# Graph and feed-forward stack on one core: the order of loads, stores and layer tiles in the first stage

## The chip, the cores and the metric

The kernel runs on one core of a Trainium2 chip. The metric is device time in microseconds (us) of one execution. A core has a matrix engine (PE, whose weight loads are listed apart as PEld), a vector engine (DVE), an activation engine (ACT), a general engine (POOL) and a synchronisation engine (SP). Transfers between device memory (DRAM) and on-chip memory are issued here from the queues of SP, ACT and POOL, and are carried out by 16 DMA engines. Each engine runs its own instructions in order. Times in the profile count from the start of the profiled span, and L12 is line 12 of the kernel.

## The reference

Four graph layers and four feed-forward blocks follow each other on 625 nodes with 512 features. Each adds its result to `x`. Only the first graph layer concerns the change:

```python
edge_index = jnp.stack([src, dst])
x = x + _L0_gnn_ref(_layernorm(x, axis=-1), edge_index, L0_gnn_W, L0_gnn_b)
x = x + _L0_ffn_ref(_layernorm(x, axis=-1)[None], ...)[0]
...
def _L0_gnn_ref(x, edge_index, W, b):
    loops = jnp.arange(n, dtype=edge_index.dtype)
    row = jnp.concatenate([edge_index[0], loops])
    col = jnp.concatenate([edge_index[1], loops])
    deg = jax.ops.segment_sum(jnp.ones(row.shape[0]), row, num_segments=n)
    dis = jax.lax.rsqrt(deg)
    norm = dis[row] * dis[col]
    h = x @ W.T + b
    out = jax.ops.segment_sum(norm[:, None] * h[row], col, num_segments=n)
    return jax.nn.relu(out)
```

There are 10,000 edges. Later graph layers use the same edges: one with the edge weights, one with the mean over the incoming edges, one with the degrees of the target nodes on both sides.

## The kernel before, in words

The 625 nodes are five tiles (`NT`) of 125 (`P`) partitions, and `x` stays on chip as `x[125, 5, 512]`. The 10,000 edges lie as 80 on each of 125 partitions. The kernel turns the edges into dense matrices of 625 by 625, `count` (number of edges) and `weighted` (sum of weights), and every graph layer is then a matrix product. The first stage, `graph_and_L0_gnn` (L369), runs in this order:

1. Loads. `Ctx.__init__` issues the load of `x` on SP's queue (L67). Then come `src` on SP (L387), `dst` on ACT (L388), the edge weights on SP (L390), the layer's weight (L464, issued by the helper at L92) and its bias (L98, on ACT).
2. Edges. DVE turns the indices into sorting keys (L392 to L409). `sort(t)` (L422) picks with MAX8 and MATCH_REPLACE8 up to 32 edges (`CAP`) of each partition whose source lies in tile t.
3. Matrices. For each tile and each of 32 slots DVE makes one-hot rows (`hot_dst` L477, `hot_src` L470), ACT makes three weighted copies of the latter (L472), and PE multiplies them into `wide` and `rest` (L497, L499). That is 640 pairs of matmuls. The sort of the next tile, and in the first tile the layer norm of `x` (`C.layernorm(xn, C.x)`, L487; its statistics are L152), are put between them.
4. A branch for left-over edges (L517) that every engine has to pass. `weighted` is stored for later (L554).
5. The tail. `degrees` makes 1/sqrt of the degrees. `turn(t)` transposes the normed `x` on PE (L609). `source_row` (L585) spreads the degrees over a row. `symmetric` (L576) makes one tile of a normalised matrix on DVE (L578, L580). `hidden(t)` is `x W + b` (PE L230, bias added by DVE, L615). `targets` (L561) sums `count` over columns on PE (L564) into `drow` (ACT L566). `layer(t)` (L619) multiplies `m0` with all five tiles of `h` (PE L213), and DVE adds the result to `x` (L622) and takes statistics (L623). `mean` (L569) makes the mean matrix (DVE L570, L571, POOL L573) and stores it (L574). `target_row` and `target_col` (L595, L599) and five more `symmetric` make `sym`, which is stored at L646. The order of the calls is written out at L625 to L647: hidden tiles, targets, then the five layer tiles with mean, target_row, target_col and sym between them.
6. The next stage, `L0_ffn` (L650), places its tiles in on-chip memory that the first stage's pool has given back. It loads expert weights into a ring (L676), norms `x` into `xn` (L161), transposes it (L173), and makes q, k, v (L237, L230) and an attention of 20 turns (L262 to L366).

The order of instructions on an engine is not quite the program's: the framework plans each engine's order with times of its own, taking what it believes ready and, among that, what stands earlier in the program. The trace shows this, for instance where DVE does L152 of the layer norm ahead of L64 and L392. Once planned, the order is fixed, and an instruction whose data is late holds up all behind it on its engine. PSUM tiles of the tail come from one pool of three buffers, named `pt`.

The three stored matrices are `[125, 5, 625]` in float32, 1525.9 KB each. Their stores go out as one transfer of 125 partitions; the later loads of the same matrices are already split in two, 112 and 13 partitions (`load_graph`, L203).

Of the kernel before, what the change touches and what calls it, by code (L numbers as in the profile page):

```python
# [28 lines left out]
N, D, P, NT = 625, 512, 125, 5  # L29
KC = D // 128  # L30
HALVES = ((0, 313), (313, 312))
# [17 lines left out]
class Ctx:  # L49


    def __init__(self, tc, ins, out, stack):
        self.tc, self.nc, self.ins, self.out = tc, tc.nc, ins, out
        nc = tc.nc
        pool = lambda name, bufs, **k: stack.enter_context(tc.tile_pool(name=name, bufs=bufs, **k))
        self.keep = pool("keep", 1)
        self.dram = pool("scratch", 1, space=DRAM)
        self.stack = stack
        self.open_mid("right")
        part = self.keep.tile([128, 1], F32, name="part")  # L60
        nc.gpsimd.iota(part, pattern=[[0, 1]], base=0, channel_multiplier=1,
                       allow_small_or_imprecise_dtypes=True)
        self.ident = self.keep.tile([128, 128], F32, name="ident")
        nc.vector.tensor_scalar(self.ident, self.iota[:, :128], part, None, op0=ALU.is_equal)  # L64
        self.ones = self.keep.tile([128, 128], F32, name="ones")
        nc.vector.memset(self.ones, 1.0)
        nc.sync.dma_start(self.x, ins["x"].rearrange("(t p) d -> p t d", p=P))  # L67

        self.graph = {
            k: self.dram.tile([P, NT, N], F32, name=f"graph_{k}") for k in ("weighted", "mean", "sym")  # L70
        }
# [130 lines left out]

    def load_graph(self, pool, kind):  # L203
        m = pool.tile([P, NT, N], F32, name=f"m_{kind}")

        for a, b in ((0, 112), (112, P)):
            self.nc.sync.dma_start(m[a:b], self.graph[kind][a:b])
        return m

    def aggregate(self, out, m, t, h, start=True, stop=True):  # L210

# [157 lines left out]
def graph_and_L0_gnn(C):  # L369
# [9 lines left out]
    nc, tc, I = C.nc, C.tc, C.ins  # L379
    W0, W1 = 512, N - 512  # L380
    with ExitStack() as st:
        E = st.enter_context
        pool = E(tc.tile_pool(name="g", bufs=1))
        T = lambda shape, name, dtype=F32: pool.tile(shape, dtype, name=name)
# [3 lines left out]
        nc.scalar.dma_start(ints[:, 1], I["dst"].rearrange("(p c) -> p c", p=P))  # L388
        ew = T([P, EC], "edge_w")
        nc.sync.dma_start(ew, I["edge_weight"].rearrange("(p c) -> p c", p=P))  # L390
        iota = T([P, N], "iota16", F16)
        nc.vector.tensor_copy(iota, C.iota[:P])  # L392
        ef = T([P, 2, EC], "edge_f")
# [67 lines left out]
        count, weighted = T([P, NT, N], "count"), T([P, NT, N], "weighted")  # L461
# [89 lines left out]
        drow, inv, trow, srow = (T([P, N], k) for k in ("drow", "inv", "trow", "srow"))  # L551
        m, sym, m0 = (T([P, NT, N], k) for k in ("m", "sym", "m0"))
        xT = T([128, KC, N], "xT")
        nc.sync.dma_start(C.graph["weighted"], weighted)  # L554


        def degrees():
# [3 lines left out]
        def targets(n0, w_):  # L561
            pr = ps.tile([128, 512], F32, name="pt")
            for s in range(NT):
                nc.tensor.matmul(pr[:P, :w_], C.ones[:P, :P], count[:, s, n0:n0 + w_],  # L564
                                 start=s == 0, stop=s == NT - 1)
            nc.scalar.copy(drow[:, n0:n0 + w_], pr[:P, :w_])  # L566


        def mean():  # L569
            nc.vector.tensor_scalar_max(inv, drow, 1.0)  # L570
            nc.vector.reciprocal(inv, inv)  # L571
            for t in range(NT):
                nc.gpsimd.tensor_mul(m[:, t], count[:, t], inv)  # L573
            nc.sync.dma_start(C.graph["mean"], m)  # L574

        def symmetric(m, t, sq, col, row):  # L576

            nc.vector.scalar_tensor_tensor(m[:, t], count[:, t], col[:, t:t + 1], row, op0=ALU.mult, op1=ALU.mult)  # L578
            diag = m[:, t, t * P:(t + 1) * P]
            nc.vector.scalar_tensor_tensor(diag, C.ident[:P, :P], sq[:, t:t + 1], diag, op0=ALU.mult, op1=ALU.add)  # L580
# [4 lines left out]
        def source_row(t):  # L585
            if t == 0:
                nc.vector.tensor_mul(ssq, scol, scol)
            dg = C.small.tile([P, P], F32, name="junk")
            nc.vector.tensor_scalar(dg, C.ident[:P, :P], scol[:, t:t + 1], None, op0=ALU.mult)
            pr = ps.tile([128, 512], F32, name="pt")  # L590
            nc.tensor.matmul(pr[:P, :P], C.ones[:P, :P], dg, start=True, stop=True)
            nc.scalar.copy(srow[:, t * P:(t + 1) * P], pr[:P, :P])


        def target_row():  # L595
            nc.vector.tensor_scalar_add(drow, drow, 1.0)
            C.rsqrt(trow, drow, [P, N])

        def target_col():  # L599
            for t in range(NT):  # L600
                junk = C.small.tile([P, P], F32, name="junk")
                nc.vector.scalar_tensor_tensor(junk, C.ident[:P, :P], 1.0, trow[:, t * P:(t + 1) * P],
                                               op0=ALU.mult, op1=ALU.mult, accum_out=tcol[:, t:t + 1])
            nc.vector.tensor_mul(tsq, tcol, tcol)
# [7 lines left out]
        def hidden(t):  # L612
            ph = ps.tile([128, 512], F32, name="pt")
            C.linear(ph[:P], xT, t, w)
            nc.vector.tensor_add(h[:, t], ph[:P], bias[:P])  # L615
# [3 lines left out]
        def layer(t):  # L619
            po = ps.tile([128, 512], F32, name="pt")  # L620
            C.aggregate(po[:P], m0, t, h)
            nc.vector.scalar_tensor_tensor(C.x[:, t], po[:P], 0.0, C.x[:, t], op0=ALU.max, op1=ALU.add)  # L622
            nc.vector.bn_stats(C.stats[:, t], C.x[:, t])  # L623
# [3 lines left out]
            turn(t)  # L627
        for t in range(NT):
            source_row(t)
        for t in range(NT):  # L630
            symmetric(m0, t, ssq, scol, srow)
            hidden(t)
        for n0, w_ in HALVES:
            targets(n0, w_)
        layer(0)
        mean()
        layer(1)
        target_row()
        layer(2)
        target_col()  # L640
        for t in (0, 1):
            symmetric(sym, t, tsq, tcol, trow)
        layer(3)
        for t in range(2, NT):
            symmetric(sym, t, tsq, tcol, trow)
        nc.sync.dma_start(C.graph["sym"], sym)  # L646
        layer(4)  # L647


def L0_ffn(C):  # L650
# [1094 lines left out]


PHASES = [graph_and_L0_gnn, L0_ffn, L1_gnn, L1_ffn, L2_gnn, L2_ffn, L3_gnn, L3_ffn]


# [48 lines left out]
```

## Time and profile before

| What | us |
|---|---|
| Median of three runs | 5357.06 |
| Lowest and highest | 5355.81, 5363.99 |
| The profiled execution's own time | 5365.64 |
| Span of its trace | 5363.8 |
| PE busy in the span | 4975.2 (93%) |
| DVE busy | 2690.5 (50%) |
| ACT busy | 1100.6 (21%) |
| First matmul starts | 27.14 |
| First PE work of `L0_ffn` starts | 280.66 |

In the page's listing, a line of the timeline has the start, the busy time, the engine, the line, the operation, the written and read tiles with their shapes, how many instructions were merged (x5), and in brackets the idle time of the engine just before it and who ended it. A letter q after an engine's name stands for its queue: the time given there is that of issuing the transfer, not of the transfer. The table by windows gives busy time and number of instructions for each engine, the granted PE clock (1.00 is full), the mean share in which the 16 DMA engines were busy, and GB/s. PE is busy through most of the span, but the averages say nothing of the first stage, which is the first twentieth of it and has its own gaps.

### The profile page before, as it was taken

The numbers are of one execution on the slowest core, as the hardware profiler recorded it, in microseconds if no ns is written. First come the engines' busy times: TensorE is split into PE (matmuls) and PEld (weight loads), VectorE is DVE, ScalarE is ACT, GpSimd is POOL, SyncE is SP. The second block draws the span as 40 slices with busy tenths as digits, with TensorE's granted clock in tenths as the row PEclk, the third lists the DMA queues.
The fourth block names the chain that finished last, engine by engine and source line by source line (L and its number), as shares of the span: only waits on it lengthen the run. The fifth ranks groups of instructions, "written<-read, shape, count | busy, mean of one in ns | idle before, by whom it ended". The sixth has DMA issues, their size and how long they took to land. (4 is left out here: it accounts for less than half of the span.)

```text
span 5363.8 us, 184920 instructions
## 1 busy us (share of the span) xinstructions
PE 4975.2 (93%) x74524; PEld 3140.2 (59%) x74524; DVE 2690.5 (50%) x13552; ACT 1100.6 (21%) x4478; POOL 61.6 (1%) x57
## 2 busy tenths in 40 slices
PE   7986999999999979999999999999999999999988
PEld 5555755555556645555555555565555655555545
DVE  6533024240025146666666656666566666656258
ACT  7433111110115111111111111111111111111125
POOL 0000000000000000000000000000000000000000
PEclk9987998989989989999999999999999999999988
DMA  1031962221116310000000000000000000000100
GB/s 37 34 109 55 319 191 73 89 65 53 45 50 214 124 39 6 7 11 6 6 6 6 6 6 6 6 6 12 7 6 6 6 6 6 6 6 0 54 27 10
DMA packets 167915, 232.19 MB, mean 43 GB/s; under 512 B 64226, under 2 KB 80983, under 8 KB 167000
## 3 DMA queue, kind: packets, MB, share of 16 engines
q1 hardware_dynamic: 155388, 220.04, 12.9%
q10 hardware_dynamic: 10122, 7.55, 0.5%
q0 software_dynamic: 2240, 2.57, 0.2%
q8 instruction: 81, 1.33, 0.1%
q14 instruction: 84, 0.69, 0.0%
HBM read 196.59 MB, written 33.54 MB: 43 GB/s over the span
## 5 line engine op out<-in xcount | busy, mean ns | idle before, releaser
L1496 PE MATMUL pa<-wp,left 128*23 128x384 bf16 x33312 | 1502.7, 327 | 129.7 <-issue 39.2
L1496 PEld LDWEIGHTS pa<-wp,left 128*23 128x23 bf16 x33312 | 811.0, 93 | 643.9 <-DVE left L1633 153.9
L1525 PE MATMUL po<-wo,left 128*1 128x128 f32 x20000 | 659.1, 273 | 0.0
L1525 PEld LDWEIGHTS po<-wo,left 128*1 128x1 f32 x20000 | 482.7, 84 | 126.6 <-issue 0.2
L1537 PE MATMUL spare<-wo,ident 128*128 128x256 f32 x1250 | 437.4, 431 | 25.2 <-issue 25.2
L1611 DVE STREAM_TRANSPOSE col<-pa 128x384 f32<-128x384 f32 x625 | 349.3, 559 | 194.5 <-PE pa L1496 194.5
L1601 DVE COPY col<-gxb 128x16 f32 x625 | 114.4, 183 | 652.0 <-DVEq L1576 652.0
L1568 ACT ACTIVATE act<-ga 128x12 f32<-128x12 f32 x625 | 132.7, 212 | 1185.7 <-DVE ga L1613 1185.7
L1563 ACT COPY xrow<-xsb 1x4 f32<-1x4 f32 x625 | 120.5, 193 | 1211.4 <-ACTq L1561 1211.4
L1537 PEld LDWEIGHTS spare<-wo,ident 128*128 128x128 f32 x1250 | 186.1, 188 | 165.7 <-issue 165.7
L1338 PE MATMUL pg<-xT,w 128*128 128x312 f32 (+1 forms) x1024 | 275.2, 429 | 1.4 <-DVE gt L1347 0.7
L1338 PEld LDWEIGHTS pg<-xT,w 128*128 128x128 f32 x1024 | 193.5, 190 | 82.6 <-DVE gt L1347 4.5
L1488 PE MATMUL lg<-wso,th 128*1 128x8 f32 x5008 | 216.2, 169 | 15.7
L1484 PE MATMUL lg<-wsel,act 128*1 128x8 f32 x5008 | 216.3, 169 | 3.1 <-DVE act L1622 1.2
L1615 DVE STREAM_TRANSPOSE col<-po 128x128 f32<-128x128 f32 x625 | 198.6, 318 | 24.6
L497 PE MATMUL wide<-hot_dst,hot_src 125*125 125x512 bf16 x640 | 178.6, 392 | 27.2 <-DVE hot_dst L477 27.1
L1488 PEld LDWEIGHTS lg<-wso,th 128*1 128x1 f32 x5008 | 147.6, 81 | 74.3 <-DVE wso L1625 12.5
L1481 PEld LDWEIGHTS lg<-xrow,ones 1*1 1x1 f32 x1252 | 51.3, 76 | 237.0 <-issue 237.0
L1625 DVE TENSOR_TENSOR wso<-wsel,so 128x32 f32<-128x32 f32 x625 | 120.2, 192 | 117.2 <-ACT so L1570 112.5
L1484 PEld LDWEIGHTS lg<-wsel,act 128*1 128x1 f32 x5008 | 147.5, 81 | 48.7 <-DVE act L1622 4.6
L230 PE MATMUL po<-w,hT 128*125 128x512 f32 x400 | 175.1, 592 | 0.0
L1570 ACT ACTIVATE so<-go 128x4 f32<-128x4 f32 x625 | 128.2, 205 | 215.3 <-DVE go L1620 215.3
(417 smaller groups left out, 6091.1 us busy)
## 6 DMA issues: line engine op xcount, KB each, us to landing
ring<-in_L_ffn_W_dram SPq DMA_DIRECT2D x64, 1024.0 KB
gxb<-gx SPq DMA_DIRECT2D x25, 800.0 KB
w<-in_L_ffn_WihT_dram SPq DMA_DIRECT2D x16, 1024.0 KB
raw<-in_L_ffn_WhhT_dram SPq DMA_DIRECT2D x24, 512.0 KB
gx<-gt SPq DMA_DIRECT2D x16, 626.0 KB
iw<-gates SPq DMA_DIRECT2D x32, 312.5 KB
gx<-gt SPq DMA_DIRECT2D x16, 624.0 KB
w<-in_L_ffn_W_dram SPq DMA_DIRECT2D x32, 256.0 KB
```

What stands on the lines that cost most here:

```text
L230: self.nc.tensor.matmul(out, xT[:, k, t * P:(t + 1) * P], w[:, k, :], start=start and k == 0, stop=stop and k == k_n - 1)
L497: nc.tensor.matmul(wide[i], hs[:, k], hd[:, :W0], start=first, stop=last)
L1338: nc.tensor.matmul(pg[:, :n], w[:, k, s * 128:(s + 1) * 128], xT[:, k, n0:n0 + n], start=k == 0, stop=k == KC - 1)
L1484: pe.matmul(lg, c2[:, s:s + 1], wsel[:, 1, s], start=False, stop=False)
L1488: m = pe.matmul(lg, th[:, s:s + 1], wso[:, s], start=False, stop=s == KC - 1)
L1496: m = pe.matmul(pa[32 * j:32 * j + 2 * GAP + 1], upper[:, s], wp[e][:, s, i, j].rearrange("p g n -> p (g n)"), start=k == 0, stop=k == 11, ...
L1525: m = pe.matmul(po[32 * j:32 * j + 1].rearrange("p (u r) -> p u r", r=32), left[:, s, 0:1], wo[e][:, s].rearrange("p (u j r) -> p j u r", ...
L1537: pe.matmul(spare[:, :256], C.ident, wo[0][:, 0, :256], start=True, stop=True)
L1568: act.activation(act4[:, 0:3].rearrange("p g s -> p (g s)"), ga, AF.Tanh, scale=0.5).then_inc(sem["ifg"])
L1570: act.activation(so, go, AF.Sigmoid).then_inc(sem["so"])
L1611: dve.transpose(col[:, :12, :32], pa.rearrange("p (b r) -> p b r", r=32)).then_inc(sem["ta"])
L1615: dve.transpose(col[:, 12:, :32], po.rearrange("p (s r) -> p s r", r=32)).then_inc(sem["to"])
```

## The change

- The load of `x` moves from `Ctx.__init__` to behind the three edge loads, and goes out as two transfers of 112 and 13 partitions. A helper `by_parts` does this, and `load_graph` now calls it too (its two transfers are the same as before).
- A copy of one column on ACT stands behind the loads; nothing reads its result.
- The stores of `weighted`, `mean` and `sym` go out as two transfers each.
- In the tail, `targets` moves ahead of the `m0` tiles. The `hidden` tiles are spread between mean, target_row, target_col and sym, and all five `layer` tiles come last, after the store of `sym`.

```diff
-        nc.sync.dma_start(self.x, ins["x"].rearrange("(t p) d -> p t d", p=P))
...
     def load_graph(self, pool, kind):
         m = pool.tile([P, NT, N], F32, name=f"m_{kind}")
+        self.by_parts(m, self.graph[kind])
+        return m
+
+    def by_parts(self, dst, src):
 
         for a, b in ((0, 112), (112, P)):
-            self.nc.sync.dma_start(m[a:b], self.graph[kind][a:b])
-        return m
+            self.nc.sync.dma_start(dst[a:b], src[a:b])
...
         nc.sync.dma_start(ew, I["edge_weight"].rearrange("(p c) -> p c", p=P))
+        C.by_parts(C.x, I["x"].rearrange("(t p) d -> p t d", p=P))
+
+        nc.scalar.copy(T([P, 1], "table"), C.ones[:P, 0:1])
...
-        nc.sync.dma_start(C.graph["weighted"], weighted)
+        C.by_parts(C.graph["weighted"], weighted)
...
-            nc.sync.dma_start(C.graph["mean"], m)
+            C.by_parts(C.graph["mean"], m)
...
         for t in range(NT):
             source_row(t)
+        for n0, w_ in HALVES:
+            targets(n0, w_)
         for t in range(NT):
             symmetric(m0, t, ssq, scol, srow)
-            hidden(t)
-        for n0, w_ in HALVES:
-            targets(n0, w_)
-        layer(0)
+        hidden(0)
         mean()
-        layer(1)
+        hidden(1)
         target_row()
-        layer(2)
+        hidden(2)
         target_col()
         for t in (0, 1):
             symmetric(sym, t, tsq, tcol, trow)
-        layer(3)
+        hidden(3)
         for t in range(2, NT):
             symmetric(sym, t, tsq, tcol, trow)
-        nc.sync.dma_start(C.graph["sym"], sym)
-        layer(4)
+        C.by_parts(C.graph["sym"], sym)
+        hidden(4)
+        for t in range(NT):
+            layer(t)
```

## The prediction

> **What bounds the kernel now.** I began with the page: PE is busy for 93% of the span, so a change helps only where PE stands idle or where its work starts later than it need. The chain of waits on the page covers only the last 370 us (from 4995), so I left it aside and read the timeline of the first 28 us and of 196 to 345 us, all engines; then the same stretches by windows of 1 us.
>
> ```profile
> 0.74 0.36 SPq L67 DMA_DIRECT2D x<-in_x_dram  x1
> 1.16 4.63 SPq L387 DMA_DIRECT2D edge_i<-in_src_dram  x1
> ...
> 5.84 0.34 SPq L390 DMA_DIRECT2D edge_w<-in_edge_weight_dram  x1
> ...
> 17.06 0.69 DVE L152 BATCH_NORM_STATS2 ln_st<-x 125x6 f32<-125x512 f32 x1 [15.96 <-DMA x<-in_x_dram]
> 17.67 0.23 DVE L394 CAST edge_f<-edge_i 125x160 f32<-125x160 int32 x1
> ...
> 26.43 0.26 DVE L470 TENSOR_SCALAR hot_src<-iota,where 125x125 bf16<-125x125 f16 x1
> ...
> 26.77 1.28 ACT L472 ACT_TABLE_LOAD   x1 [26.77 <-DVE hot_src L470]
> ...
> 27.14 0.58 PE L497 MATMUL wide<-hot_dst,hot_src 125*125 125x512 bf16 x1 [27.14 <-DVE hot_dst L477]
> ```
>
> DVE stands still for 15.96 us until `x` is there, because its order has a statistics instruction of `x` ahead of the edge work. The edges are queued behind `x`, and only from 17.67 does their work run, for 9 us, to the first one-hot row and the first matmul. From about 37 us on DVE waits for PE at each slot (98 waits, 51.5 us, by the view of waits), so the 640 pairs of matmuls run at PE's pace, 0.2745 us a pair, to 205.9. A start that is earlier by some time therefore ends this phase earlier by the same time.
>
> ```profile
> 8.00:9.00 1.00, 0.00 (x0) 0.00 (x0) 0.00 (x0) 0.00 (x0) 0.00 (x0) 1.00 0.34 129
> ...
> 19.00:20.00 1.00, 0.00 (x0) 0.00 (x0) 1.00 (x6) 0.00 (x0) 0.00 (x0) 1.00 1.05 387
> ...
> 277.00:278.00 1.00, 0.00 (x0) 0.00 (x0) 0.00 (x0) 0.00 (x0) 0.00 (x0) 0.50 0.35 150
> 278.00:279.00 1.00, 0.00 (x0) 0.00 (x0) 0.00 (x0) 0.00 (x0) 0.00 (x0) 0.50 0.18 75
> ```
>
> The last two columns: while `x` alone moves, a third of the DMA engines is busy at 129 GB/s; the weights behind it (128 partitions) fill all of them at 387. The store of `sym` at 277 looks like the load of `x`. The tail, by the timeline (DVE and PE):
>
> ```profile
> 218.91 17.33 PE L230 MATMUL pt<-w,xT 128*125 128x512 f32 x40
> 236.08 5.42 PE L564 MATMUL pt<-count,ones 125*125 125x313 f32 x20
> 241.34 21.62 PE L213 MATMUL pt<-h,m 125*125 125x512 f32 x50
> 280.66 1.90 PE L173 MATMUL pt<-ident,xn 125*128 125x125 f32 x8 [17.70 <-DVE xn L161]
> ```
>
> ```profile
> 242.51 4.07 DVE L571 RECIPROCAL inv<-inv 125x625 f32<-125x625 f32 x1
> ...
> 265.86 0.68 DVE L622 SCALAR_TENSOR_TENSOR x<-pt,x 125x512 f32<-125x512 f32 x1
> ...
> 268.80 0.17 DVE L124 TENSOR_TENSOR ln_r<-ln_r,rs_s 125x5 f32<-125x5 f32 x1
> 279.55 2.72 DVE L161 TENSOR_SCALAR xn<-x,ln_mv,ln_r 125x512 f32<-125x512 f32 x5 [10.59 <-DMA graph_sym<-sym]
> ```
>
> PE works without a break to 262.96 and then idles 17.70 us. Of that, 2.9 us are DVE finishing `sym` before it gets to the last tile of `x` (265.86), 3.1 us are the statistics chain to 268.97, 10.59 us are DVE's wait for the store of `sym` to be read out of memory that `xn` is laid over, and 1.1 us the first norm until PE has data.
>
> **What the Trainium skill says.** "DMA: Bandwidth & Descriptors", section "Why a DMA increments its semaphore by 16 and not by 1", says that a transfer from SP or ACT runs on the largest number of engines up to 16 that divides the leading dimension: 125 partitions give 5, 112 give 16, 13 give 13. The trace agrees: 5 of 16 is 0.31, and 0.30 to 0.35 is seen for `x` and the stores. Its section "Queues, rings and completion order" says that each queue has one ring per engine, taken in order; agreeing, `src` lands only behind `x`, and its issue took 4.63 us instead of 0.34. "TensorE: Matmul & The Clock Gate", section "What's actually happening", has the PE clock halve after an idle window of about 3.4 us. Here it fell at about 265.85, 2.9 us after PE stopped, and at 211.05, 5.2 us after. "SBUF — State Buffer", section "Who interferes with whom", says that a POOL instruction and some DVE ones lock each other out; L596 took 1.48 us beside POOL's L573, against 0.48 for the like L123.
>
> **The change part by part.** *Start.* With `x` out of the way the edges are issued at 0.74 and 1.10 on SP and at 0.74 on ACT. First bytes came about 1.1 us after issue for `x`, a completion takes about 0.9 us (the store of `sym` stops halfway through 278 to 279, DVE goes at 279.55), and the small rows need about 0.6 us: I estimate 3.3 us. `x` is issued at about 1.44 and 1.8. With the 256 KB bias beside it, 1.54 MB at 387 GB/s need 4.0 us; 2.5 + 4.0 + 0.9 = 7.4 us, where 17.0 was seen. The order on DVE decides what this brings, and the trace shows it for the old program only: there three statistics stand ahead of L64 and L392, which need only iota rows that POOL had made by 1.6 us. So the plan believes the iota late, about 1.4 to 2.1 us after `x`. `x` now comes a little later in any plan (two small transfers more ahead of it), so it likely still precedes the iota, with one or two statistics in between instead of three. Bounds: no statistics ahead, then 3.3 us plus the 8.76 us from L394 to L470 less two statistics of 0.6 gives 10.8; the whole layer norm ahead, then 7.4 + 5 x 0.6 statistics + 1.9 for aggregates and root + 2.5 for L161 + 6.5 for the rest gives 21.3. I take two statistics: from 17.06 to 26.43 are 9.37 us; less one statistics (0.6) and less the part of the edge chain that has been done while waiting (0.85: L394, L397, three L399, L400), 7.9 us after 7.4, so 15.3 instead of 26.43: 11.1 us. The statistics that move between matmuls fall into DVE's waits there and cost nothing.
>
> The copy on ACT draws the 1.28 us table load at 26.77 to the start, where ACT is idle until 26. PE had covered most of it with another slot's first pair (a matmul at 27.78 without ACT's data), so I take 0.5 us, bounds 0 and 1.28. Start: 11.6 us, bounds 4.8 and 16.9.
>
> *Stores in two parts.* `weighted` and `mean` have no one waiting. `sym` needs about 1.56 MB / 387 GB/s = 4.0 us plus 2 instead of 13.6. One issue more is 0.3 us on SP, idle at these points; what stands behind on SP is the load of Wv, needed at 321, and the ring, needed after the attention.
>
> *Order of the tail.* PE's work is the same: turns and source rows to 218.91, targets 5.42 to 224.3, hidden 17.33 to 241.7, layers 21.62 to 263. Whether PE gets its data is DVE's matter, in old-clock times: `m0` (five times 0.8 + 0.26) 219.4 to 224.7; `drow` from ACT at 224.8; L570 and L571 to 229.3; h(0) 0.6 to 229.9; L596 1.4 (beside POOL) to 231.3; h(1) to 231.9; root on ACT, reciprocal 4.0 to 236.3; h(2) to 236.9; four instructions of 2.6 and h(3) 0.6 to 240.1; target_col 1.1 to 241.2; sym 5 x 1.06 to 246.5; h(4) to 247.1. hidden(4) is ready at 241.7, but its addition stands behind `sym` in the program. PE can do the first four fifths of layer(0) meanwhile (3.45 us, to 245.1), then waits 2.0 us, or none if the plan interleaves layer(1). The hidden tiles find free `pt` buffers throughout (hidden(3) needs h(0)'s, free at 229.9, wanted at 234.7). Behind the waiting h(4) on DVE is nothing but the layers. After the last layer DVE has only `x`, statistics and root: 3.1 + 1.1 + 0.05 = 4.25 us of gap where 17.70 were. `sym` has long been stored, so the 10.59 us go, and what is late next is this DVE chain. Gain 13.45 - 2.0 = 11.4 us; bounds 0.4 (third rival) and 15.4. In this short gap the clock may not fall: it stood at half from 280.66 to 286.1, about 2 us of loss, which I don't count but put into the upper bound.
>
> Sum: 11.6 + 11.4 = 23.0 us. The profiled execution took 5365.64 (1.8 of it outside the span) and would be 5342.6; it was 8.6 us above the median. The difference is taken from the median: 5357.06 - 23 = 5334.
>
> **The rivals.**
> *Nothing gated by x.* No statistics ahead of the edges (start 26.43 - 10.8 + 0.5 = 16.1), layers without a stall (13.4): 29.5 us, 5327.5, or 5325.5 if the clock holds. For it: three statistics ahead were a close call of some 2 us; against: two-part transfers may also come earlier in the plan.
> *The whole layer norm first.* If the plan believes `x` much sooner than the iota: 26.43 - 21.3 + 0.5 = 5.6, with 11.4: 17 us, 5340. Against it: `x` comes behind the edges.
> *DVE bounds the tail.* All five additions of h stand behind mean, root and sym: 224.8 + 19.3 = 244.1, three `pt` buffers let PE do three hidden tiles before, two more (6.9) plus the adding follow, and layers end 10.3 us late, with the clock lost once more (2.7): 0.4 instead of 11.4, total 12 us, 5345. For it: DVE has 24 us of work beside 23 us of PE's; against: the old order took L622 of layer(0) as soon as the reciprocal let it.
> *Both at once*, the change does not do what it says: 5.6 + 0.4 = 6 us, 5351, no difference to be told.
> *Slower: the next stage is planned differently.* The stage after is planned in one go with this one, and a turn of its attention takes 4.2 us (L277 at 358.06, 362.28, 366.46) except one that came 3.48 us late (374.13, after PE L266). If the new plan puts such a stall into 12 of the 20 turns, it costs 42 us: +19, 5376. It evens out at 7 stalls. Against it: the turns' own order depends on each other, not on when the stage starts.
>
> **How the numbers follow.** A measurement of this kernel tells about 0.2% (10.7 us) from no change. Chances: forecast 0.45, nothing gated 0.25, layer norm first 0.10, DVE bound 0.08, both 0.06, slower 0.06. The first four are faster (two points off for the DVE bound's edge): 0.86; same 0.08; slower 0.06. The range of 5324 to 5348 holds the first four with 2 us of scatter at the low end and 3 at the high one.
>
> **What would show it.** First matmul near 16 us instead of 27.14, with DVE's first wait ended by `x` near 7.4 (right) or by the edges near 3.3 (first rival). DMA share near 1.0 while `x` moves. No table load at the first L472. L213 in one run of 21.6 us, or with a stall of about 2 us before its fifth product; the addition L615 of the last tile behind the last L580. The gap before the first L173 about 4.3 us, ended by DVE with no store in it. The prediction is wrong if DVE still waits for a DMA beyond 12 us, if PE idles over 5 us between L564 and L213, or if the attention's turns change.

## The result, and the profile after

| What | before | after |
|---|---|---|
| Median of 12 runs each, side by side, us | 5363.18 | 5343.33 |
| Lowest and highest, us | 5355.81, 5374.44 | 5325.14, 5348.00 |
| Profiled execution (its span), us | 5365.64 (5363.8) | 5344.59 (5342.8) |
| First matmul, us | 27.14 | 12.54 |
| First PE work of `L0_ffn`, us | 280.66 | 252.84 |

The ratio of after to before is 0.9955, with a 95% interval of 0.9946 to 0.9965: 19 to 29 us less. One of the 12 runs of after took 10682.92 us; it is counted in the median (5342.15 without it), but in neither the ratio nor the range. In the code after, the copy on ACT is L395, `by_parts` L210, `hot_src` and `hot_dst` L475 and L482, the matmul pair L502 and L504, the addition of `h` L620, the layers L215, and the transposes in the next stage L172.

The timeline of the start of after (start, busy time, engine, line, operation, and in brackets the idle time before it and who ended it):

```profile
1.34 1.28 ACT L395 ACT_TABLE_LOAD   x1 [1.34 <-PEq L1794]
...
3.51 0.24 DVE L399 CAST edge_f<-edge_i 125x160 f32<-125x160 int32 x1 [2.42 <-DMA edge_i<-in_src_dram]
...
5.29 0.28 DVE L64 TENSOR_SCALAR ident<-iota,part 128x128 f32<-128x128 f32 x1
...
12.54 0.59 PE L502 MATMUL wide<-hot_dst,hot_src 125*125 125x512 bf16 x1 [12.54 <-DVE hot_dst L482]
...
24.24 0.69 DVE L151 BATCH_NORM_STATS2 ln_st<-x 125x6 f32<-125x512 f32 x1
```

DVE waits 2.42 us, for the edges, and not for `x` at all; the first one-hot row (L475) starts at 11.84. The first statistic of `x` (L151) stands at 24.24, among the matmuls, where DVE had waits to spare. The last of the 640 pairs ends at 190.4 (205.9 before): the lead, 14.6 us at the first matmul, is 15.5 at the end of the phase. The next matmul, which counts the left-over edges, shows it, in before and then in after:

```profile
205.82 0.19 PE L513 MATMUL wide<-ones,nlate 125*1 125x1 f32 x2
```

```profile
190.30 0.19 PE L518 MATMUL wide<-ones,nlate 125*1 125x1 f32 x2
```

The tail of after, the timeline of PE, and below it that of DVE around the last hidden tile:

```profile
196.83 4.40 PE L614 MATMUL pt<-ident,xn 125*128 125x125 f32 x20 [6.34 <-DVE scol L119]
...
208.60 17.33 PE L232 MATMUL pt<-w,xT 128*125 128x512 f32 x40
225.76 5.32 PE L215 MATMUL pt<-h,m 125*125 125x512 f32 x12
231.94 16.57 PE L215 MATMUL pt<-h,m 125*125 125x512 f32 x38 [0.86 <-DVE h L620]
252.84 1.39 PE L172 MATMUL pt<-ident,xn 125*128 125x125 f32 x7 [4.33 <-issue]
```

```profile
231.20 0.68 DVE L620 TENSOR_TENSOR h<-pt,bias 125x512 f32<-125x512 f32 x1
231.80 0.34 DVE L585 SCALAR_TENSOR_TENSOR sym<-ident,tsq,sym 125x125 f32<-125x125 f32 x1
```

The gap ahead of the next stage is 4.33 us instead of 17.70. The layers stop once, for 0.86 us, since the last addition of `h` stands behind nearly all of `sym`: only the last piece of its diagonal (L585) comes after it. From the matmul of the left-over edges to the first PE work of `L0_ffn`, before took 74.84 us and after takes 62.54. The stage thus gains 15.5 us at the start and 12.3 us in the tail, 27.8 in all; the span gains 21.0. (DVE's first instruction behind the branch, at 212.14 in before and 196.02 in after, would make this 16.1 and 11.7, but it is no steady mark: in a second profile of before it came at 211.26.) The windows of after while `sym` is stored (the last three columns are PE clock, DMA share and GB/s) have the 16 engines full in the middle of the store, where before had a third:

```profile
234.00:236.00 2.00, 2.00 (x6) 0.85 (x5) 1.03 (x3) 0.00 (x0) 0.00 (x0) 1.00 0.99 331
```

### The profile page after: what moved, and what is told of

The parts are those of the page before. It is cut to its first block, busy times and chain, and to the rows that moved or that the text cites. A ratio compares the mean times of both kernels' runs of the same rounds, so it can differ in the third digit from the quotient of the medians.

```text
span 5342.8 us, 184932 instructions
## 1 busy us (share of the span) xinstructions
PE 4977.2 (93%) x74524; PEld 3136.7 (59%) x74524; DVE 2688.4 (50%) x13552; ACT 1100.5 (21%) x4479; POOL 61.5 (1%) x57
## 5 line engine op out<-in xcount | busy, mean ns | idle before, releaser
L1543 PE MATMUL spare<-wo,ident 128*128 128x256 f32 x1250 | 437.4, 431 | 25.5 <-issue 25.5
L502 PE MATMUL wide<-hot_dst,hot_src 125*125 125x512 bf16 x640 | 177.8, 391 | 12.5 <-DVE hot_dst L482 12.5
```

The costliest lines, as they stand in the source:

```text
L502: nc.tensor.matmul(wide[i], hs[:, k], hd[:, :W0], start=first, stop=last)
L1543: pe.matmul(spare[:, :256], C.ident, wo[0][:, 0, :256], start=True, stop=True)
```

## The experiments

Three questions were open. Which part of the edit moves the start? Is the tail's gain due to the order of the work or to the quicker stores? Where do the 6.8 us go that the profile of after loses between `L0_ffn` and the end? The theories in the expectations were set up after the result was seen. Runs of one program differ by up to 24 us in the end, so a kernel that was run once is read by its marks in the first stage. In the three kernels that were profiled twice the start of `L0_ffn` repeats within 0.2 us (after), 0.35 (before) and 0.9 (the kernel of experiment 3).

### 1. The edges first, and nothing else

`edges_first_only`, from before:

```diff
-        nc.sync.dma_start(self.x, ins["x"].rearrange("(t p) d -> p t d", p=P))
...
         nc.sync.dma_start(ew, I["edge_weight"].rearrange("(p c) -> p c", p=P))
+        nc.sync.dma_start(C.x, I["x"].rearrange("(t p) d -> p t d", p=P))
```

> The kernel before with one edit: the load of x, still one transfer of 125 partitions, is issued behind the three edge loads. Theory (the order of the loads alone makes the early start): DVE's first wait ends with the edges at about 3.5 us, the first matmul is at 12.5 to 13.2 instead of 27.14, and the one-hot matmuls end about 14 to 15 us earlier (near 191). Rival (x must also come fast, because statistics of x stand ahead of the edge work or between its first instructions): DVE waits for x until about 17.5 and the first matmul is at 24 to 27.

Its timeline, DVE and the first matmul:

```profile
3.83 0.24 DVE L394 CAST edge_f<-edge_i 125x160 f32<-125x160 int32 x1 [2.74 <-DMA edge_i<-in_src_dram]
...
21.49 1.29 DVE L151 BATCH_NORM_STATS2 ln_st<-x 125x6 f32<-125x512 f32 x2 [15.81 <-DMA x<-in_x_dram]
22.70 0.27 DVE L64 TENSOR_SCALAR ident<-iota,part 128x128 f32<-128x128 f32 x1
...
29.94 0.59 PE L497 MATMUL wide<-hot_dst,hot_src 125*125 125x512 bf16 x1 [29.94 <-DVE hot_dst L477]
```

The rival is right, and it is worse than the rival said: the first matmul comes 2.8 us later than before. The edges are there at 3.83 and DVE begins with them, but two statistics of `x` stand ahead of L64. DVE stops at 5.7 us and waits 15.81 us for an `x` that, issued later and beside the weights, lands at 21.49. To load the edges first is by itself a loss in this stage: `L0_ffn` starts at 283.37, 2.7 us later than before. The time of the one run, 5361.6, can't tell this.

### 2. `x` in two parts, and nothing else

`x_in_parts_only`, from before:

```diff
-        nc.sync.dma_start(self.x, ins["x"].rearrange("(t p) d -> p t d", p=P))
+        for a, b in ((0, 112), (112, P)):
+            nc.sync.dma_start(self.x[a:b], ins["x"].rearrange("(t p) d -> p t d", p=P)[a:b])
```

> The kernel before with one edit: x is still loaded first, but as 112 and 13 partitions. Theory (5 of 16 DMA engines were the limit): x lands near 6.5 us, the edges right behind it, and the first matmul is at about 17, so 10 us of the gain at the start come from the split alone. Rival (the wait was for the edges' place in the queue, not for the width of the transfer): first matmul above 24.

The timeline of DVE, and the first matmul:

```profile
1.61 0.49 DVE L64 TENSOR_SCALAR ident<-iota,part 128x128 f32<-128x128 f32 x1 [0.51 <-POOL part L61]
...
11.20 0.69 DVE L153 BATCH_NORM_STATS2 ln_st<-x 125x6 f32<-125x512 f32 x1 [8.56 <-DMA x<-in_x_dram]
...
21.05 0.58 PE L498 MATMUL wide<-hot_dst,hot_src 125*125 125x512 bf16 x1 [21.05 <-DVE hot_dst L478]
```

Neither expectation is met. The first matmul is 6.1 us earlier than before, about what the quicker `x` gives (11.20 instead of 17.06), but `x` lands far later than the 6.5 expected, and a statistic still stands ahead of the edges (L395 follows at 11.82). The split changed DVE's order as well: L64 and the other iota work now come first, and four statistics are mixed into the edge chain. The time was 5364.63.

### 3. `x` whole, but issued one load later

`x_whole_later` and `x_whole_later_timed` are one kernel: `edges_first_only` with the same line issued behind the weights of the layer. On SP's queue that is one place later; in the program it is some 95 lines later, behind the sort of the first tile.

```diff
-        nc.sync.dma_start(C.x, I["x"].rearrange("(t p) d -> p t d", p=P))
...
             for step in sort(0):
                 step()
+            nc.sync.dma_start(C.x, I["x"].rearrange("(t p) d -> p t d", p=P))
```

> The kernel before with one move: the load of x, whole, is issued from the edge phase, behind the weights of the layer (third on SP, after the edges), and nothing else. The DVE order of this program has the whole edge chain, L64 and the iota row ahead of the first statistic of x. Theory (what decides the start is whether a statistic of x stands ahead of the iota work in DVE's order, not how x is transferred): first wait of DVE ends with the edges near 3.8, first matmul between 12.3 and 13.2 instead of 27.14, first PE work of L0_ffn near 266 (280.66 less 14.5), with the gap of 17.7 ahead of it as before. Rival (the transfer in two parts is needed, since x whole keeps a queue busy until 21): the first matmul comes at 20 or later, or DVE waits several us for x among the first matmuls and the phase ends less than 10 us earlier.

The timeline of `x_whole_later`:

```profile
3.22 0.24 DVE L393 CAST edge_f<-edge_i 125x160 f32<-125x160 int32 x1 [2.12 <-DMA edge_i<-in_src_dram]
5.00 0.28 DVE L64 TENSOR_SCALAR ident<-iota,part 128x128 f32<-128x128 f32 x1
...
12.26 0.58 PE L497 MATMUL wide<-hot_dst,hot_src 125*125 125x512 bf16 x1 [12.26 <-DVE hot_dst L476]
```

The theory is right. The same undivided load, one place further back on SP, has no statistic ahead of the iota work, and the first matmul comes at 12.26, against 29.94 in experiment 1 and 12.54 in after. `L0_ffn` starts at 265.18, 15.5 us before the kernel before. So the start needs no transfer in two parts; it needs an order in which nothing waits for `x`. How the framework comes to put the statistics there isn't in the trace; that the order differs is.

This run ended at 5364.12, no better than before. One run can't settle it, so the kernel was run more often:

> The kernel of x_whole_later, timed: in its one look the start gained 15.5 us and the end 1.5 beside the profile of before. Theory (the loss was that run's clock): the median lies 10 to 18 us below that of before, ratio 0.9966 to 0.9982. Rival (the earlier start alone is given back in this program): ratio 0.9990 or more.

The median of 17 runs is 5354.20 (5342.53 to 5361.51), against 5366.93 for before beside it (22 runs, 5352.89 to 5376.48); the ratio is 0.9975, interval 0.9968 to 0.9983, or 9 to 17 us. The gain of the start does reach the end; the two profiled executions, 5364.12 and 5361.51, lie above and at the upper end of this kernel's spread.

### 4. Without the copy on ACT

`no_table_copy`, from after:

```diff
-        nc.scalar.copy(T([P, 1], "table"), C.ones[:P, 0:1])
```

> The kernel after without the copy on ACT that draws the table load to the start. Theory (PE covers most of the load with the first pair of another slot, as the prediction argued): the table load of 1.28 us comes back between the first one-hot row and its first scaling, the first matmul stays at 12.5 within 0.2, and the last one-hot matmul ends 0 to 0.7 us later than the 190.4 of the kernel after. Rival (it is all on the path): 1.2 to 1.4 us later.

The timeline of ACT at the first one-hot row:

```profile
12.25 1.28 ACT L476 ACT_TABLE_LOAD   x1 [12.25 <-DVE hot_src L474]
```

The load is back where it was in before, and costs nothing: the first matmul is at 12.62, and the last matmul of the phase (L517, the number of left-over edges) at 190.39, where after has 190.30. Both differ by the same 0.08 to 0.09, less than the difference between two profiles of one kernel. The copy is worth nothing that can be seen. The time was 5343.25.

### 5. The stores in two parts, with the old order of the tail

`stores_in_parts_only`, from before, and the same for `weighted` and `mean`:

```diff
-        nc.sync.dma_start(C.graph["sym"], sym)
+        for a, b in ((0, 112), (112, P)):
+            nc.sync.dma_start(C.graph["sym"][a:b], sym[a:b])
```

> The kernel before with one edit: the three matrices are stored as 112 and 13 partitions, the order of the tail as before. Theory: sym is issued at 266, is out after about 6 us instead of 13.6, and the first work of the next stage on PE starts about 7.5 us earlier, so the gap is about 10 us instead of 17.70. Rival (the store of the mean matrix or another release holds xn): the gap stays at 17 or more.

The timeline at the end of the stage:

```profile
272.56 2.58 DVE L161 TENSOR_SCALAR xn<-x,ln_mv,ln_r 125x512 f32<-125x512 f32 x5 [4.34 <-DMA graph_sym<-sym]
...
273.52 1.90 PE L173 MATMUL pt<-ident,xn 125*128 125x125 f32 x8 [11.31 <-DVE xn L161]
```

The wait for the store shrinks from 10.59 to 4.34 us and the gap from 17.70 to 11.31: 6.4 us, where 7.5 had been expected. From its issue at 265.22 the store takes about 7.3 us to free the memory, instead of 13.6. The time was 5359.37.

### 6. The new order of the tail, with the stores whole

`stores_whole`, from after, and the same for `weighted` and `mean`:

```diff
-        C.by_parts(C.graph["sym"], sym)
+        nc.sync.dma_start(C.graph["sym"], sym)
```

> The changed kernel with one edit undone: the three matrices are stored as one transfer each. Theory (the order of the tail alone removes the wait, since sym is issued at 232 and even 13.6 us end before xn is wanted at 252): the gap ahead of the next stage stays at 4.3 us and its first PE work at 252.8, within 0.5. Rival (the split removes the wait): DVE waits for the store again and the gap is 6 us or more.

The timeline of POOL, ACT, its queue and DVE at the end of the stage:

```profile
250.72 0.52 POOL L689 MEMSET zero<- 128x512 f32 x1 [29.34 <-DMA graph_sym<-sym]
250.76 0.35 ACTq L97 DMA_DIRECT2D bias<-in_L_ffn_bo_dram  x1
...
251.67 0.51 ACTq L97 DMA_DIRECT2D ln_g<-in_L_ffn_ln_g_dram  x1
252.23 0.21 ACT L118 ACTIVATE rs_s<-ln_v 125x5 f32<-125x5 f32 x1 [35.35 <-POOL zero L689]
...
252.47 0.19 DVE L119 RECIPROCAL ln_r<-rs_s 125x5 f32<-125x5 f32 x1 [1.80 <-ACT rs_s L118]
```

Neither expectation is met: the gap is 5.73 us instead of 4.33. The store, issued at 232.45 and moving at about a third of the engines (0.31, 123 GB/s in the windows), is out at about 250.6, 1.8 us after the layers end. It no longer holds DVE itself. It holds the loads of three biases and scales on ACT's queue (issued from 250.76 on, the first and the last of them shown), whose memory comes free with it, as POOL's does; ACT's root of the variance stands behind them in program order, and DVE waits 1.80 us for that root. The two parts are thus worth 1.4 us in the new order, and 6.4 in the old one. The new order alone does most of the tail's work. The time was 5348.72.

### 7. The same two kernels once more

`after_again` and `before_again` change nothing.

> The kernel after, unchanged, once more. Theory (what the first stage gains is the same in each run, and what the later stages give back is the granted clock, which falls differently from run to run): first PE work of L0_ffn at 252.84 within 0.3; the distance from there to the end of the span differs by 2 us or more from the 5090.0 of the first profile, and where it differs, the clock stands at half at another place. Rival (the give-back belongs to the program): the same distance within 1 us, with the half clock in the same windows, near 801 to 820 and 5196 to 5238. Time 5343 within 6, 0.995 to 0.997 of the kernel before.

> The kernel before, unchanged, once more, for where its later stages lose time. Theory (the clock falls differently from run to run): first PE work of L0_ffn at 280.66 within 0.3 as in the first profile, and the rest of the span differs from it by some us, with the half clock at other places of the last attention (the first profile had it full there) or of L1_ffn. Rival (what the program does decides it): the same marks within 1 us to the end of the span.

`after_again` reached `L0_ffn` at 252.64 and took 5085.7 us from there to the end of its span, against 5090.0 in the first profile. `before_again` reached it at 280.31, 0.35 us earlier than the first profile where 0.3 had been the bound, and took 3.5 us less from there. `after_again` has a ratio of 0.9955 to before (interval 0.9942 to 0.9968, medians 5342.33 and 5365.06); `before_again` took 5361.66. The table has the lead of each profiled run over the first profile of before, in us, where the same PE work was found near the place (time in before):

| Place in before | 283 | 806 | 856 | 4980 | 5220 | end |
|---|---|---|---|---|---|---|
| after | 27.7 | 26.8 | 23.2 | 25.6 | 24.3 | 21.0 |
| after_again | 27.9 | 27.5 | 27.5 | 29.1 | 28.7 | 25.5 |
| before_again | 0.5 | 3.1 | 1.8 | 4.0 | 4.0 | 3.9 |
| x_whole_later_timed | 14.6 | 15.1 | 11.6 | 6.4 | 6.5 | 4.1 |

The windows of `L1_ffn` in the three profiles, over the same work as far as their leads tell, first before, then after, then `after_again` (the third column from the end is the PE clock):

```profile
825.00:855.00 30.00, 29.72 (x133) 23.18 (x132) 14.92 (x107) 5.16 (x10) 0.00 (x0) 0.76 0.03 11
```

```profile
798.00:828.00 30.00, 29.72 (x125) 25.55 (x125) 12.80 (x104) 5.12 (x10) 0.00 (x0) 0.64 0.00 1
```

```profile
797.00:827.00 30.00, 29.72 (x134) 23.46 (x133) 15.02 (x108) 5.16 (x10) 0.00 (x0) 0.75 0.02 9
```

PE is busy for 29.72 us in all three and gets less done where the clock is lower: 3.6 us lost in after between 806 and 856, nothing in `after_again`, the same program. All thirteen profiles kept of this case agree: this stretch took 49.7 to 53.4 us, and the more of it stood at half clock (32.6 to 40.2 us), the longer it took. This bears the theory out for `L1_ffn`. In the last attention it fails, as there the two profiles of one program don't differ: both profiles of after lose about 3 us between 5220 and the end, and the two of before lose nothing. This loss too is mostly clock: from that place on the same 726 matmuls keep PE busy for 121.0 us at a mean clock of 0.81 in after, and for 117.9 at 0.84 in before.

It isn't a property of the edit's instructions, which lie 4,900 us earlier, and not of one part of the edit either. Of the thirteen profiles, the three that come to this place at most about 4 us ahead of the first profile of before (both of before, and `edges_first_only`) lose nothing there. The ten that come 6.5 us or more ahead lose 2.4 to 10.1, among them `x_in_parts_only` (6.7 us ahead, 5.7 lost), `stores_in_parts_only` (9.9 and 3.6) and, with most, `stores_whole` (27.0 and 10.1). So the loss goes with an earlier arrival, but not in proportion to it, and why the clock falls so isn't shown.

### 8. Further in the same direction

PE idles 6.34 us at the branch, though the transposes of the normed `x` have their data, and 0.86 us for the last hidden tile. `all_early`, from after, in short:

```diff
+        xT = T([128, KC, N], "xT")
...
+            pst = st2.enter_context(tc.tile_pool(name="g_pst", bufs=2, space=PSUM))
...
+            for t in range(NT):
+                turn(t)
...
-        for t in range(NT):
-            turn(t)
-        for t in range(NT):
-            source_row(t)
         for n0, w_ in HALVES:
             targets(n0, w_)
+        for t in range(NT):
+            source_row(t)
...
         hidden(3)
+        hidden(4)
...
         C.by_parts(C.graph["sym"], sym)
-        hidden(4)
```

> The kernel after with three moves more: the transposes of the normed x ahead of the branch on the late edges (in a PSUM pool of their own), the target sums ahead of the source rows, and the last hidden tile ahead of the last three tiles of the symmetric matrix. Theory (in the kernel after PE idles 6.34 us at the branch, where the transposes of 4.4 us have all their data, and 0.86 us for the last hidden tile): 4.2 to 5.5 us less than after, first PE work of L0_ffn at 247.3 to 248.7 instead of 252.84, no stall within the layers; time some 5 us below that of the kernel after beside it. Rival (DVE is the engine that bounds this part, 24 us of work beside 23 of PE): PE waits as much later on, in the hidden tiles or the layers, and L0_ffn starts at 251.5 or later.

The timeline of PE, then of POOL and of DVE, and at last that of DVE in after for the same instructions, with POOL idle:

```profile
220.99 8.74 PE L232 MATMUL pt<-w,xT 128*125 128x512 f32 x16 [4.39 <-DVE h L624]
...
255.53 1.90 PE L172 MATMUL pt<-ident,xn 125*128 125x125 f32 x8 [4.34 <-issue]
```

```profile
209.76 8.61 POOL L588 TENSOR_TENSOR m<-count,inv 125x625 f32<-125x625 f32 x5 [207.74 <-DVE inv L586]
```

```profile
209.58 2.80 DVE L593 SCALAR_TENSOR_TENSOR m<-count,scol,srow 125x625 f32<-125x625 f32 x2
212.31 2.88 DVE L595 SCALAR_TENSOR_TENSOR m<-ident,ssq,m 125x125 f32<-125x125 f32 x2
215.11 3.92 DVE L593 SCALAR_TENSOR_TENSOR m<-count,scol,srow 125x625 f32<-125x625 f32 x2
```

```profile
205.40 0.60 DVE L585 SCALAR_TENSOR_TENSOR m<-ident,ssq,m 125x125 f32<-125x125 f32 x2
205.92 1.64 DVE L583 SCALAR_TENSOR_TENSOR m<-count,scol,srow 125x625 f32<-125x625 f32 x2
```

The rival is right: `L0_ffn` starts 2.7 us later than in after. With the targets first, the reciprocal of `mean` comes ahead of the `m0` tiles, so POOL's five products (209.76 to 218.4, 8.61 us instead of 7.18 in after) run beside them, and the slowed instructions are those that lie in this time. A pair of L593 takes 2.80 and 3.92 us where after needs 1.65, a pair of L595 2.88 instead of 0.60: 5.7 us more on DVE. PE fills its three `pt` buffers with hidden tiles and waits 4.39 us for the first addition. The median of 6 runs was 5345.40, ratio 0.9961 (0.9947 to 0.9974), the same as after's within the interval.

`turns_early` is `all_early` with the targets back behind the source rows.

> The kernel after with the transposes of the normed x ahead of the branch, in a PSUM pool of their own, and the last hidden tile ahead of the last three tiles of the symmetric matrix; the targets stay behind the source rows, where all_early had moved them ahead. Theory (all_early lost because the mean's reciprocal and POOL's products came ahead of the scaled count on DVE): no stall in the hidden tiles, layers in one run, first PE work of L0_ffn at 249.5 to 250.9 instead of 252.84, of the 4.4 us of transposes some 2 to 3 us kept, since DVE's chain from the branch to the last hidden tile takes over. Rival (the clock takes it back: PE idles over 4 us behind the transposes, so that the targets run at half speed): 252 or later. The time can't tell 2 us from nothing; the trace of the stage can.

Its timeline of PE:

```profile
198.95 3.14 PE L606 MATMUL pt<-junk,ones 125*125 125x125 f32 x10 [5.44 <-DVE junk L604]
201.89 6.08 PE L579 MATMUL pt<-count,ones 125*125 125x313 f32 x20
...
224.97 21.63 PE L215 MATMUL pt<-h,m 125*125 125x512 f32 x50
250.95 1.87 PE L172 MATMUL pt<-ident,xn 125*128 125x125 f32 x8 [4.35 <-issue]
```

The layers run in one piece and `L0_ffn` starts at 250.95, 1.9 us before after's 252.84 and 0.05 past what was expected. Of the 4.40 us of transposes most goes back at once: PE still waits 5.44 us for the first `junk`, and source rows and targets take 1.3 us more, as the half clock falls on them now instead of on the transposes. The median of 6 runs is 5343.30, ratio 0.9958 (0.9943 to 0.9973). The trace shows the 1.9 us; the time doesn't tell this kernel from after.

## Why the prediction was right, and where it was not

The forecast, 5334 us within 5324 to 5348, was a gain of 23.0 us; the median after is 5343.33. Of the 9.3 us between, 6.1 are the reference: before has 5363.18 over 12 runs, where its first three gave 5357.06. Against the profiled execution the prediction had said 5342.6, and 5344.59 came. That closeness is in part luck, since two errors nearly cancel: the stage was taken 4.8 us too small (27.8 came), and 6.8 us that the later stages lost in this profile were not foreseen. By what happened in the stage, the rival "nothing gated by x" with its 29.5 us was nearer (1.7 us off) than the forecast.

*The start was mis-sized, and the likeliest order on DVE was the wrong one.* "I take two statistics", said the step, with `x` at 7.4 us, and so 15.3 for the first one-hot row; it came at 11.84, with no statistics ahead. This is the rival "nothing gated by x", which had 10.8. By the end of the phase the start gained 15.5 us, where 11.6 had been forecast and 16.1 in that rival. Of the 3.9 us more, the order on DVE gave 3.5; 0.5 goes off, since the table load gave nothing; and 0.9 came within the phase, where an earlier start was to end it "earlier by the same time". Of this 0.9 up to 0.65 can be scatter: so far apart are the two profiles of experiment 3 between the same two matmuls. (The lower bound of the start, by its own terms, is 5.1 and not 4.8.) Experiments 1 and 3 show that this term is a switch: the same load at an earlier or a later place makes the first matmul 29.94 or 12.26. An order read from the trace of one program was not evidence for that of the next.

*The landing of `x` was estimated too early.* With 387 GB/s for all bytes the step had 7.4. With two parts and `x` still first, it landed at 11.20, though the engines were full (172 GB/s at a share of 1.10 from 7 to 10 us of that run): a full share was not a full rate. The small rows that move beside it don't explain this. Packets under 2 KB made 0.17 of that share; those of 2 KB took 197 ns each, where those of the weights alone took 88 (18 to 21 us of before). Why isn't shown. In after this lies off the path.

*The edges*: estimated at 3.3, seen at 3.51 in after, 3.22 to 3.83 in the others that load them first. Right.

*The table load*: 0.5 was taken, within 0 to 1.28. It is nothing (experiment 4), as PE covers all of it. The argument was right, the value too high.

*The tail*: 11.4 was forecast, and 12.3 came (74.84 us less 62.54; 74.75 less 62.44 in `before_again` and `after_again`). The gap was to be 4.25 and is 4.33. The last `h` was to stand behind `sym` and cost 2.0 us, or none if the plan interleaved the next layer tile; the plan put two products of it in (12 matmuls ahead of the stall; a product shows as two of them, and four fifths of the first tile are 8), and 0.86 was left. These 1.1 us are the term that was mis-sized. That "the 10.59 us go" since the store is early was right, and so was what is late next, DVE's chain of statistics and root. The quicker store was to need 6 us, and needs 7.3 in experiment 5. "In this short gap the clock may not fall": it fell all the same, at 253.2, and stood at half until 260.0 in after (265.7 to 286.2 in before), so nothing was gained there. Experiment 6 adds what the step left out: with the stores whole, not DVE but ACT's queue would have been late next.

*DVE bounds the tail* and *slower, by the attention* were false. The first came true in `all_early`, by another way: POOL beside the `m0` tiles. The attention of `L0_ffn` keeps its pace: the lead is 27.1 us at 480, behind it.

*What nobody forecast*: from 27.8 us at `L0_ffn` to 21.0 at the end of the profile. The prediction ended its sum at the stage. In `L1_ffn` this is the granted clock of that run; in the last attention it is mostly the clock too, and why it falls there with an earlier arrival is open (experiment 7). The interval of the ratio, 19 to 29 us, allows that on the mean nothing is given back; experiment 7 makes a loss of some us in the last attention the likelier.

## What to carry to other kernels

An engine with a fixed order is as late as the latest input among its first instructions: before a load is moved, look at which instruction of which engine waits for it, and after it is moved look again, since an order planned by a framework may change with the place of one line (12.26 or 29.94 us here). Where a store's memory is used by the next stage, give it work to hide behind before making it quicker: the order alone brought the gap from 17.70 to 5.73 us, the quicker store alone to 11.31, both to 4.33. And where single runs of one program differ by more than the effect, measure at the end of the stage in the trace, by a mark that repeats between profiles of one kernel, and let many runs speak for the rest.

## What the runs showed of the hardware

- A busy DMA engine isn't a fast one. In after the engines were at a share of 1.03 between 3 and 11 us, and moved 205 GB/s, with edges, bias, `x` and weights in flight; the weights alone had 387 GB/s at 1.05 in before. The packets of 2 KB took 165 ns each in after, against 88 for the weights alone.
- The PE clock fell to half at the branch in after too (0.50 from 196 to 202 us by the windows, in a gap of 6.34), at the end of its short gap of 4.33, when PE had just resumed, and in `turns_early` in one of 5.44. The falls came 4.7, 4.7 and 2.9 us after PE's last matmul. This agrees in kind with the Trainium skill, "TensorE: Matmul & The Clock Gate", section "What's actually happening", which has the clock fall after an idle window of about 3.4 us; the last of the three, by the modelled end of the matmul, is shorter than that window. Moving work ahead of such a gap moves the half-speed time on to what comes next.
- POOL's products slow DVE's scaled counts (L593 in `all_early`) by 1.7 to 2.4 times (2.80 and 3.92 us a pair instead of 1.65), the short ones on the diagonal (L595) by nearly five (2.88 instead of 0.60), and L601 in after by three (1.48, where the same instruction behind the products, L611 in `all_early`, took 0.47); the reciprocal beside the same products in after stayed at 4.07.
- A late store can hold an engine that never touches it: the loads that need its memory wait in that engine's own queue, ahead of its arithmetic (1.80 us in `stores_whole`).
